# Layer 0's experts: the first product with stationary weights, its output features along the partitions

## The chip, the cores and the metric

The kernel runs on one core of one Trainium2 chip. The metric is the device time of one execution in microseconds (us). The times of the kernel before are those of ten executions: median 4035.64 us, lowest 4032.58, highest 4039.06. The engines are named as in the profile: PE is TensorE's matmul pipe, PEld its weight loads, DVE VectorE, ACT ScalarE, POOL GpSimd, SP SyncE. ACTq and SPq are the queues of ACT and SP where they issue transfers.

## The reference

A graph network with 6250 nodes of 256 features is computed in four parts, each added to the running `x`: a weighted graph convolution with a small dense head, a mixture of eight experts, a relational graph layer, and a second mixture of six experts. The change lies in the second part alone:

```python
def _moe(tokens, router_w, w1, b1, w2, b2):     # tokens: layernorm of x, 6250 x 256
    logits = tokens @ router_w.T
    probs = softmax(logits); rw, re = top_k(probs, 2); rw = rw / rw.sum(-1)
    out = tokens
    for e in range(8):
        h = gelu(tokens @ w1[e] + b1[e], approximate=False)
        y = h @ w2[e] + b2[e]
        out = out + combine[:, e:e + 1] * y
    return out
```

All numbers are float32, and both weight arrays are 8 x 256 x 256.

## The kernel before

The work runs in stages, one after another: lists of edges; messages of the first graph layer; their sums, with the dense head, the router and the sending of tokens woven in; the experts of layer 0; the table of the second graph layer; its sums with the experts of layer 1 woven in; and a last stretch with the remaining experts of layer 1.

**How tokens reach the experts.** The router picks two experts for each token, and each token's row is written by an indirect DMA to two places of an array `xs` in HBM, grouped by expert. Experts' regions are cut into tiles of 128 rows, of which there are at most TE = 105 in all, so every tile belongs to one expert. Which expert it is and where the tile begins in `xs` is known only when the program runs: the numbers are read into registers, eight tiles at a time (`blocks_of`, L1394 and L1395), on SP for the place and on PE and DVE for the expert.

**The stage of the experts (L1384 to L1451).** `in_stages` runs five functions as a software pipeline over the 105 tiles. In round i it calls them from the last to the first, each on an older tile:

- `finish(i-4)`: the second product. The transposed hidden rows are the stationary operand, and the expert's `fw2` (256 columns, at an address from a register) moves. DVE adds the bias `fb2` (L1448), and ACT's queue issues the 128 KB transfer to `ys` (L1449).
- `across(i-3)`: two PE transposes of the hidden rows (L234) and an ACT copy out of PSUM to `fhT` (L236).
- `hidden(i-2)`: the first product. The transposed tokens `fxT` are stationary, `fw1` moves (L1428). DVE adds `fb1` along the free axis (L1432), and ACT applies Gelu to the 128 x 256 result (L1433).
- `into(i-1)`: two PE transposes of the tokens (L234) and an ACT copy to `fxT` (L236).
- `fetch(i)`: SP loads 128 rows of `xs` (L1400).

I write F, A, H and T for the PE work of `finish`, `across`, `hidden` and `into`. A float32 matmul shows in the profile as two MATMUL rows, here called halves: F and H have four halves of 256 columns each. A float32 transpose shows as one row, so A and T have two rows of 128 columns each.

**Buffers.** The pool `experts` has three buffers for each of `fx`, `fxT`, `fh`, `fhT` and two for `fy`. PSUM tiles of F and H come from a pool of four banks, those of A and T from a pool of two.

**What sets the order.** The framework puts each engine's instructions into one list when the program is compiled. It starts from the order in which the program writes them, may put a later instruction ahead of an earlier one that its plan sees waiting, and adds the waits. On the chip each engine goes through its list in order. In the steady part of this stage PE's list is F, A, H, T, as written.

**Around the stage.** Before it, `rows_of("L0_ffn_b1")` and `rows_of("L0_ffn_b2")` (L1305, L1306; DMA issued at L1110) spread the two bias arrays over all partitions. `cols`, a 128 x 48 array that is made at the start of the program, holds other biases and `L0_ffn_b1` as columns, 128 features along the partitions. After the stage, `combine` (L1469, L1475) gathers rows of `ys` with indirect DMAs, adds them to `X`, and the table of the second graph layer (L1509) begins.

Other lines that the prediction uses: L239 (two ACT activations of 128 x 128, one for each half of a PSUM tile that two transposes filled, in the dense head of layer 0), and L246 with L253 and L1091 (the experts of layer 1, whose first two products have the weights stationary and whose last group is a single tile of 128 rows).

Of the kernel before, what the change touches and what calls it, by code (L numbers as in the profile page):

```python
# [8 lines left out]
F32 = mybir.dt.float32  # L9
# [5 lines left out]
AF = mybir.ActivationFunctionType  # L15
# [5 lines left out]
D = 256  # L21
# [19 lines left out]
TE = (2 * N + 8 * 127) // 128  # L41
# [16 lines left out]
def gnn_ffn_kernel(ctx: ExitStack, tc: tile.TileContext, a, out):  # L58
    nc = tc.nc
# [7 lines left out]
    def psum_mm(name):  # L67
        return p_mm.tile([128, 512], F32, tag="mm", name=name)
# [81 lines left out]
    col0, n = {}, 0  # L150
    for name in (
# [8 lines left out]
        k = math.prod(ap.shape) // 128  # L160
# [4 lines left out]
    cols = const.tile([128, 48], F32, name="cols")  # L165
# [5 lines left out]
    def load_w(pool, name, tag=None):  # L171
        w = pool.tile([128, 2, a[name].shape[1]], F32, name=f"w_{name}", tag=tag or f"w_{name}")
        nc.sync.dma_start(w, a[name].rearrange("(k p) f -> p k f", p=128))
        return w

    def blocks_of(blk, t0, engines, top):
        _, v = nc.values_load_multi_w_load_instructions(
            blk[0:1, t0 : t0 + 8],
            engines=engines,
            min_val=0,  # L180
            max_val=top,
            skip_runtime_bounds_check_because="it is counted or bounded",
        )
        return v
# [45 lines left out]
    def transpose_to(name, dest, x, bias=None):  # L230

        pt = p_tr.tile([128, 2, 128], F32, tag="tr", name=f"pt_{name}")
        for k in range(2):
            nc.tensor.transpose(pt[:, k, :], x[:, k * 128 : (k + 1) * 128], ident)  # L234
        if bias is None:
            nc.scalar.copy(dest, pt)  # L236
        else:
            for k in range(2):
                nc.scalar.activation(dest[:, k, :], pt[:, k, :], AF.Relu, bias=bias[k])  # L239
# [23 lines left out]
    w = load_w(xp0, "L0_gnn_W", "x_out")  # L263
# [97 lines left out]
    with tc.If(unsorted > 0):  # L361
        with tc.tile_pool(name="reorder", bufs=1) as rp:
# [3 lines left out]
            for i, (name, dt) in enumerate((("src", I32), ("edge_weight", F32), ("edge_type_8", I32))):  # L366
                e = rp.tile([EP, EC], dt, name=f"e_{name}", tag="e")
# [153 lines left out]
    for b in range(NT):  # L521
        for h in range(2):
# [4 lines left out]
                start=(b == 0),  # L527
                stop=(b == NT - 1),
# [124 lines left out]
    for c0 in range(0, TN, DCH):  # L653
# [21 lines left out]
        for c in range(DCH):  # L675
# [4 lines left out]
                start=(c0 + c == 0),  # L680
                stop=(c0 + c == TN - 1),
# [414 lines left out]
    def load_experts(pool, name):  # L1096
        n_e = a[name].shape[0]
        w = pool.tile([128, n_e, 2, D], F32, name=f"w_{name}")
        for e in range(n_e):
            nc.sync.dma_start(w[:, e], a[name][e].rearrange("(k p) f -> p k f", p=128))  # L1100
        return w


    def rows_of(name, pool):

        v = a[name]
        k = math.prod(v.shape)
        r = pool.tile([128, k], F32, name=f"rows_{name}")
        flat = v.rearrange("(o n) -> o n", o=1) if len(v.shape) == 1 else v.rearrange("e (o n) -> o (e n)", o=1)
        nc.sync.dma_start(r, flat.to_broadcast([128, k]))  # L1110
        return r
# [5 lines left out]
    fw1 = fp.tile([128, 8, 2, D], F32, name="fw1")  # L1117
# [184 lines left out]
        sum_and_send("e", True)  # L1302
    fp2 = ffn0.enter_context(tc.tile_pool(name="ffn0b", bufs=1, side="right"))
    fw2 = load_experts(fp2, "L0_ffn_w2").rearrange("p e k f -> p (e k f)")
    fb1 = rows_of("L0_ffn_b1", fp2)  # L1305
    fb2 = rows_of("L0_ffn_b2", fp2)  # L1306
    fw1 = fw1.rearrange("p e k f -> p (e k f)")

    def in_stages(stages, items):

        held = [None] * len(stages)
        for i in range(len(items) + len(stages) - 1):
            for k in reversed(range(len(stages))):
                if 0 <= i - k < len(items):
                    held[k] = stages[k](*(held[k - 1] if k else items[i]))
# [75 lines left out]
    with tc.tile_pool(name="experts", bufs=3) as xp:  # L1391
        state = {}

        def fetch(i):  # L1394
            if i % 8 == 0:  # L1395
                state["place"] = blocks_of(places, i, [ENG.SP], 8 * CAP)
                state["expert"] = blocks_of(experts, i, [ENG.PE, ENG.DVE], 7)
            e, at = state["expert"][i % 8], state["place"][i % 8]
            x = xp.tile([128, D], F32, name=f"fx{i}", tag="fx")
            nc.sync.dma_start(x, xs[bass.ds(at, 128), :])  # L1400
            if i in (30, 40):
                k = (i - 30) // 10
                nc.scalar.dma_start(
                    wr[:, k], a["L1_gnn_weight"][:, k * 128 : (k + 1) * 128, :].rearrange("r p o -> p r o")
                )
            if i == 50:
                nc.scalar.dma_start(wl, a["L1_gnn_loop_weight"].rearrange("(k p) f -> p k f", p=128))
            if i % 2 == 0 and i // 2 < NT:
                t = i // 2
                nc.gpsimd.tensor_scalar(  # L1410
                    X[:, t, :],
                    X[:, t, :],
                    stretch[:, t : t + 1],
                    offset[:, t : t + 1],
                    op0=OP.mult,
                    op1=OP.add,
                )
            return i, e, x

        def into(i, e, x):  # L1420
            xT = xp.tile([128, 2, 128], F32, name=f"fxT{i}", tag="fxT")
            transpose_to(f"fx{i}", xT, x)
            return i, e, xT

        def hidden(i, e, xT):
            ps = psum_mm(f"pf1_{i}")
            for k in range(2):
                nc.tensor.matmul(  # L1428
                    ps[:, :D], xT[:, k, :], fw1[:, bass.ds(e * 2 * D + k * D, D)], start=(k == 0), stop=(k == 1)
                )  # L1430
            h = xp.tile([128, D], F32, name=f"fh{i}", tag="fh")
            nc.vector.tensor_add(h, ps[:, :D], fb1[:, bass.ds(e * D, D)])  # L1432
            nc.scalar.activation(h, h, AF.Gelu)  # L1433
            return i, e, h

        def across(i, e, h):
            hT = xp.tile([128, 2, 128], F32, name=f"fhT{i}", tag="fhT")
            transpose_to(f"fh{i}", hT, h)
            return i, e, hT

        def finish(i, e, hT):
            ps = psum_mm(f"pf2_{i}")
            for k in range(2):
                nc.tensor.matmul(  # L1444
                    ps[:, :D], hT[:, k, :], fw2[:, bass.ds(e * 2 * D + k * D, D)], start=(k == 0), stop=(k == 1)
                )
            y = xp.tile([128, D], F32, name=f"fy{i}", tag="fy", bufs=2)
            nc.vector.tensor_add(y, ps[:, :D], fb2[:, bass.ds(e * D, D)])  # L1448
            nc.scalar.dma_start(ys[i * 128 : (i + 1) * 128, :], y)  # L1449

        in_stages([fetch, into, hidden, across, finish], [(i,) for i in range(TE)])  # L1451
    ffn0.close()


# [38 lines left out]
    for gi, t, i in tiles:  # L1493
        if i == 0 and gi + 1 < len(TABLE_GROUPS):
            stats[gi + 1] = combine(*TABLE_GROUPS[gi + 1])
        xT = ready.pop(t)
        h = hp.tile([128, NR, 3, D], BF16, name=f"hx{t}", tag="hx")
# [8 lines left out]
        for r in range(0, NR, 2):  # L1506
            ps = psum_mm(f"phx{t}_{r}")
            for k in range(2):
# [4 lines left out]
                    start=(k == 0),  # L1513
                    stop=(k == 1),
# [11 lines left out]
        ps = psum_mm(f"plo{t}")  # L1526
# [219 lines left out]
```

## Time and profile before

| what | value |
|---|---|
| median of ten executions | 4035.64 us |
| the profiled execution | 4036.39 us |
| its span in the profile | 4034.6 us |
| PE busy | 3438.2 us, 85% of the span |
| stage of the experts, first `fx` issue to last `ys` issue | 2020.6 to 2290.2 us, 269.6 us |
| PE busy between 2100 and 2150 us | 48.92 of 50 us |
| DVE, ACT, POOL busy there | 17.42, 21.56, 0 us |
| TensorE clock granted there | 1.00 |
| one tile, steady | 2.36 us |

Times in the profile are microseconds from the start of the span. A row of a timeline gives the start, the time taken, the engine, the line, the operation, the output and the inputs with their shapes, a count, and in brackets how long the engine was idle before and what ended that. A busy share of PE near 100% doesn't say that PE is at its best, since the end of a matmul is modelled and includes the way through the array.

### The profile page before, as it was taken

The numbers are of one execution on the slowest core, as the hardware profiler recorded it, in microseconds if no ns is written. First come the engines' busy times: TensorE is split into PE (matmuls) and PEld (weight loads), VectorE is DVE, ScalarE is ACT, GpSimd is POOL, SyncE is SP. The second block draws the span as 40 slices with busy tenths as digits, with TensorE's granted clock in tenths as the row PEclk, the third lists the DMA queues.
The fourth block names the chain that finished last, engine by engine and source line by source line (L and its number), as shares of the span: only waits on it lengthen the run. The fifth ranks groups of instructions, "written<-read, shape, count | busy, mean of one in ns | idle before, by whom it ended". The sixth has DMA issues, their size and how long they took to land.

```text
span 4034.6 us, 53283 instructions
## 1 busy us (share of the span) xinstructions
PE 3438.2 (85%) x14649; PEld 2300.1 (57%) x14649; DVE 2036.6 (50%) x5609; ACT 1320.0 (33%) x3006; POOL 2252.2 (56%) x2450
## 2 busy tenths in 40 slices
PE   7968877777777688888789779996789999999999
PEld 5756666656666355555467534442456666666556
DVE  6872111111111577777723387664556666666552
ACT  3714333333333233333234335662112222221213
POOL 1007777777777455555420285335777777777740
PEclk9989998998999889999899889997899999999999
DMA  4435333333333555555433354446555555555530
GB/s 122 167 109 169 126 128 126 128 128 129 130 127 124 215 180 191 191 191 191 162 127 109 98 189 196 193 198 219 150 144 151 154 152 153 150 150 150 146 106 9
DMA packets 227434, 602.88 MB, mean 149 GB/s; under 512 B 40620, under 2 KB 121689, under 8 KB 207276
## 3 DMA queue, kind: packets, MB, share of 16 engines
q0 software_dynamic: 100736, 295.11, 23.2%
q1 hardware_dynamic: 108242, 287.41, 20.5%
q10 hardware_dynamic: 18138, 16.68, 1.2%
q8 instruction: 132, 2.16, 0.2%
q14 instruction: 186, 1.52, 0.1%
HBM read 362.97 MB, written 236.11 MB: 148 GB/s over the span
## 4 chain that ended last, share of the span: by engine, by line
PE 46%; DVE 14%; DMA 8%; issue 6%; POOL 3%; ACT 2%; DVEq 1%; POOLq 0%; ACTq 0%; SPq 0%
PE ph_e1a L246 6%; DMA msgs<-msgn,at 6%; PE pa1a L1012 6%; PE py1a L1091 6%; PE ph_e2a L246 5%; PE pxn L908 4%; DVE acc L985 4%; PE pa0e L983 4%; PE phx L1509 4%; PE pf L1428 2%; PE pf L1444 2%; DVE rest L1519 2%; POOL msgs L926 1%; DVE acc L1016 1%; PE pt_fh L234 1%
## 5 line engine op out<-in xcount | busy, mean ns | idle before, releaser
L1004 POOL DMA_INDIRECT g1a<-hx,idxT x830 | 826.2, 995 | 322.6 <-PE pa1a L1012 146.5
L908 PE MATMUL pxn<-acc,sTn 128*128 x3128 | 795.2, 415 | 238.9 <-DVE sTn L891 230.7
L926 POOL DMA_INDIRECT msgs<-msgn,at x782 | 783.0, 1001 | 270.6 <-DMA msgs<-msgn,at 138.1
L908 PEld LDWEIGHTS pxn<-acc,sTn 128*128 128x128 f32 x3128 | 618.2, 207 | 415.0 <-DVE sTn L891 264.6
L983 PE MATMUL pa0e<-g0e,m0e 128*128 128x256 f32 x1660 | 482.3, 425 | 132.5 <-POOL m0e L970 64.6
L923 ACT ACTIVATE msgn<-pxn,ewT 128x256 f32<-128x256 f32 x782 | 370.1, 473 | 645.9 <-PE pxn L908 487.3
L1016 DVE TENSOR_TENSOR acc<-acc,pa1a 128x256 f32 x830 | 347.3, 418 | 343.4 <-PE pa1a L1012 312.0
L983 PEld LDWEIGHTS pa0e<-g0e,m0e 128*128 128x128 f32 x1660 | 284.4, 201 | 295.8 <-issue 117.0
L899 DVE COPY msgn<-srcT 128x32 f32<-128x32 f32 x98 | 18.1, 188 | 825.6 <-DMA msgs<-msgn,at 709.2
L1012 PE MATMUL pa1a<-g1a,m1a 128*128 128x256 bf16 x2490 | 375.4, 283 | 54.1 <-DMA g1a<-hx,idxT 38.5
L985 DVE TENSOR_TENSOR acc<-acc,pa0e 128x256 f32 x830 | 347.6, 419 | 142.3 <-PE pa0e L983 100.9
L970 POOL TENSOR_SCALAR m0e<-minus,keye 128x128 f32<-128x128 f32 x414 | 250.7, 621 | 280.8 <-PE pa0e L983 127.8
L1012 PEld LDWEIGHTS <-m1a 128*128 128x128 bf16 x2490 | 243.5, 100 | 277.2 <-issue 191.1
L1509 PE MATMUL phx<-wr,xT 128*128 128x512 f32 x784 | 369.2, 615 | 28.7 <-DVE rest L1519 20.8
L1091 PE MATMUL py1a<-w_L_ffn_expert_w,v2a 128*128 128x256 f32 x1176 | 285.5, 383 | 6.0 <-DVE acc L1016 3.0
L246 PE MATMUL ph_e1a<-xT3a,w_L_ffn_expert_w 128*128 128x512 f32 (+2 forms) x672 | 289.1, 557 | 0.0
L253 ACT ACTIVATE v1a<-ph_e1a,cols 128x512 f32<-128x512 f32 (+2 forms) x168 | 106.5, 634 | 539.3 <-PE ph_e1a L246 539.1
L246 PE MATMUL ph_e2a<-v1a,w_L_ffn_expert_w 128*128 128x512 f32 (+2 forms) x672 | 280.0, 542 | 2.1 <-DVE acc L1016 1.3
L1509 PEld LDWEIGHTS phx<-wr,xT 128*128 128x128 f32 x784 | 148.2, 197 | 189.1 <-issue 162.7
L1469 POOL DMA_INDIRECT y<-ys,ats x98 | 96.6, 986 | 277.9 <-issue 263.4
L1091 PEld LDWEIGHTS py1a<-w_L_ffn_expert_w,v2a 128*128 128x128 f32 x1176 | 208.4, 190 | 43.8 <-ACT v2a L253 10.1
L1092 DVE SCALAR_TENSOR_TENSOR X<-py1a,C1a,X 128x256 f32<-128x256 f32 x294 | 139.1, 482 | 111.4 <-PE py1a L1091 110.4
(649 smaller groups left out, 4325.9 us busy)
## 6 DMA issues: line engine op xcount, KB each, us to landing
g0e<-msgs SPq DMA_DIRECT2D x104, 1040.0 KB
hx<-hx SPq DMA_DIRECT2D x49, 1536.0 KB
rowsn<-lane_rows SPq DMA_DIRECT2D x98, 256.0 KB
fx<-xs SPq DMA_DIRECT2D x105, 128.0 KB
ys<-fy ACTq DMA_DIRECT2D x105, 128.0 KB
g1a<-hx,idxT POOLq DMA_INDIRECT x830, 3.1
msgs<-msgn,at POOLq DMA_INDIRECT x782, 2.4
msgs<-none SPq DMA_DIRECT2D x10, 650.0 KB
```

The source lines that it names most:

```text
L246: nc.tensor.matmul(ps[:, :ncols], w[:, k, f * 128 : (f + 1) * 128], xT[:, k, :ncols], start=(k == 0), stop=(k == 1),)
L908: nc.tensor.matmul(come, sT[:, k, j, :], acc[:, bass.ds(blocks[j] * D + k * D, D)], start=(k == 0), stop=(k == 1),)
L923: nc.scalar.activation(msg[:, j, :D], come, AF.Copy, scale=ewT[:, t0 + j : t0 + j + 1])
L926: ins = nc.gpsimd.indirect_dma_start(out=msgs, out_offset=bass.IndirectOffsetOnAxis(ap=at[:, t0 + j : t0 + j + 1], axis=0), in_=msg[:, j, ...
L970: nc.gpsimd.tensor_scalar(m[:, j], minus, key[:, j : j + 1], None, op0=OP.is_equal)
L983: nc.tensor.matmul(ps[:, :D], m[:, j, :], g[:, j, :D], start=True, stop=True)
L985: nc.vector.tensor_add(here, here, ps[:, :D])
L1004: nc.gpsimd.indirect_dma_start(out=g, out_offset=None, in_=table, in_offset=bass.IndirectOffsetOnAxis(ap=idxT[:, t0 + j : t0 + j + 1], axi ...
L1012: nc.tensor.matmul(ps[:, :D], m[:, j, :], g[:, k * D : (k + 1) * D], start=(k == 0), stop=(k == 2))
L1016: nc.vector.tensor_add(here, here, ps[:, :D])
L1091: nc.tensor.matmul(ps[:, :D], hT[:, k, j : j + 128], w[:, k, :], start=(k == 0), stop=(k == 1))
L1509: nc.tensor.matmul(ps, xT[:, k, :], wr[:, k, r : r + 2, :].rearrange("p r o -> p (r o)"), start=(k == 0), stop=(k == 1),)
```

## The change

`hidden` takes the weights as the stationary operand and the transposed tokens as the moving one, so that its result has features along the partitions, in two blocks of 128 features by 128 tokens in one PSUM tile. That is the form in which `finish` needs it: `across` is gone, with its two transposes and its copy. The bias now stands along the partitions, so ACT's Gelu takes it as its bias operand, reads PSUM itself and writes `fhT`, in two instructions, one for each block; the DVE add and the array `fb1` are gone. The stationary operand is no longer read at an address from a register: `into` copies the expert's weights (128 x 512) and its two bias columns (128 x 2) with DVE into tiles of their own, `fw` and `fb`, three buffers each.

```diff
@@ -1302,7 +1302,6 @@
     fw2 = load_experts(fp2, "L0_ffn_w2").rearrange("p e k f -> p (e k f)")
-    fb1 = rows_of("L0_ffn_b1", fp2)
     fb2 = rows_of("L0_ffn_b2", fp2)
@@ -1420,22 +1419,28 @@
         def into(i, e, x):
             xT = xp.tile([128, 2, 128], F32, name=f"fxT{i}", tag="fxT")
             transpose_to(f"fx{i}", xT, x)
-            return i, e, xT
-
-        def hidden(i, e, xT):
+            b1 = xp.tile([128, 2], F32, name=f"fb{i}", tag="fb")
+            nc.vector.tensor_copy(b1, cols[:, bass.ds(e * 2 + col0["L0_ffn_b1"], 2)])
+            w = xp.tile([128, 2 * D], F32, name=f"fw{i}", tag="fw")
+            nc.vector.tensor_copy(w, fw1[:, bass.ds(e * 2 * D, 2 * D)])
+            return i, e, xT, w, b1
+
+        def hidden(i, e, xT, w, b1):
             ps = psum_mm(f"pf1_{i}")
-            for k in range(2):
-                nc.tensor.matmul(
-                    ps[:, :D], xT[:, k, :], fw1[:, bass.ds(e * 2 * D + k * D, D)], start=(k == 0), stop=(k == 1)
-                )
-            h = xp.tile([128, D], F32, name=f"fh{i}", tag="fh")
-            nc.vector.tensor_add(h, ps[:, :D], fb1[:, bass.ds(e * D, D)])
-            nc.scalar.activation(h, h, AF.Gelu)
-            return i, e, h
-
-        def across(i, e, h):
+            for f in range(2):
+                for k in range(2):
+                    nc.tensor.matmul(
+                        ps[:, f * 128 : (f + 1) * 128],
+                        w[:, k * D + f * 128 : k * D + (f + 1) * 128],
+                        xT[:, k, :],
+                        start=(k == 0),
+                        stop=(k == 1),
+                    )
             hT = xp.tile([128, 2, 128], F32, name=f"fhT{i}", tag="fhT")
-            transpose_to(f"fh{i}", hT, h)
+            for f in range(2):
+                nc.scalar.activation(
+                    hT[:, f, :], ps[:, f * 128 : (f + 1) * 128], AF.Gelu, bias=b1[:, f : f + 1]
+                )
             return i, e, hT
@@ -1448,7 +1453,7 @@
-        in_stages([fetch, into, hidden, across, finish], [(i,) for i in range(TE)])
+        in_stages([fetch, into, hidden, finish], [(i,) for i in range(TE)])
```

More of the change, by code (lines that the diff above doesn't have):

```diff
@@ L1422, in into @@
             transpose_to(f"fx{i}", xT, x)
-            return i, e, xT
-        def hidden(i, e, xT):
-            ps = psum_mm(f"pf1_{i}")
-            for k in range(2):
-                nc.tensor.matmul(
-                    ps[:, :D], xT[:, k, :], fw1[:, bass.ds(e * 2 * D + k * D, D)], start=(k == 0), stop=(k == 1)
-                )
-            h = xp.tile([128, D], F32, name=f"fh{i}", tag="fh")
-            nc.vector.tensor_add(h, ps[:, :D], fb1[:, bass.ds(e * D, D)])
-            nc.scalar.activation(h, h, AF.Gelu)
-            return i, e, h
-        def across(i, e, h):
-            hT = xp.tile([128, 2, 128], F32, name=f"fhT{i}", tag="fhT")
-            transpose_to(f"fh{i}", hT, h)
+            b1 = xp.tile([128, 2], F32, name=f"fb{i}", tag="fb")
[4 more added lines that the diff above has]
+        def hidden(i, e, xT, w, b1):
+            ps = psum_mm(f"pf1_{i}")
+            for f in range(2):
[7 more added lines that the diff above has]
+                    )
+            hT = xp.tile([128, 2, 128], F32, name=f"fhT{i}", tag="fhT")
+            for f in range(2):
+                nc.scalar.activation(
+                    hT[:, f, :], ps[:, f * 128 : (f + 1) * 128], AF.Gelu, bias=b1[:, f : f + 1]
+                )
             return i, e, hT
```

## The prediction

> **What bounds the kernel now.** The page comes first. PE is the busiest engine, and in the chain that ended last the two products of the experts (L1428, L1444) have 4% of the span and the transposes of `fh` (L234) 1% more.
>
> ```profile
> PE 3438.2 (85%) x14649; PEld 2300.1 (57%) x14649; DVE 2036.6 (50%) x5609; ACT 1320.0 (33%) x3006; POOL 2252.2 (56%) x2450
> ```
>
> Then the stage's own windows (length, busy time of PE, PEld, DVE, ACT, POOL, granted clock, DMA share, GB/s):
>
> ```profile
> 2100.00:2150.00 50.00, 48.92 (x246) 36.67 (x247) 17.42 (x41) 21.56 (x61) 0.00 (x0) 1.00 0.35 111
> ```
>
> PE is full, at full clock; DVE and ACT are idle for over half, POOL wholly. The next stage gathers from `ys` and begins after the last `ys` transfer, so what the stage gains or loses passes on whole. The timeline of one steady tile shows how:
>
> ```profile
> 2274.05 0.38 PE L234 MATMUL pt_fx<-ident,fx 128*128 128x128 f32 x2
> 2274.27 1.03 PE L1444 MATMUL pf<-w_L_ffn_w,fhT 128*128 x4
> 2274.32 0.42 DVE L1432 TENSOR_TENSOR fh<-pf,rows_L_ffn_b 128x256 f32<-128x256 f32 x1 [0.91 <-PE pf L1428]
> 2274.79 0.42 ACT L1433 ACTIVATE fh<-fh 128x256 f32<-128x256 f32 x1
> 2275.26 0.20 PEld L234 LDWEIGHTS pt_fh<-ident,fh 128*128 128x128 f32 x2 [0.37 <-ACT fh L1433]
> 2275.27 0.44 PE L234 MATMUL pt_fh<-ident,fh 128*128 128x128 f32 x2
> 2275.54 1.03 PE L1428 MATMUL pf<-fw,fxT 128*128 x4
> 2276.41 0.38 PE L234 MATMUL pt_fx<-ident,fx 128*128 128x128 f32 x2
> ```
>
> Take differences of PE's starts: T 0.22, F 0.86, a hole of 0.14, A 0.27, H 0.87: 2.36 us. The hole is A waiting for Gelu (2274.79 + 0.42 = 2275.21): add and Gelu stand one after the other between H and A. A takes 0.27 where T takes 0.22, since PE refills after a wait: 0.05.
>
> One other wait is regular, once in eight tiles (waits in 2045 to 2290: total us, times, longest):
>
> ```profile
> PEld pf L1428 <- DVE fy L1448: 7.7, 13, 0.6
> ```
>
> These are the tiles where new registers are read.
>
> **The change part by part.**
>
> *A goes*: 0.27 + 0.14 = 0.41 per tile on PE, all on the path. Its ACT copy goes too, on an engine that waits anyway.
>
> *H turns*: eight halves of 128 columns instead of four of 256. The last group of layer 1 has this form:
>
> ```profile
> 4007.60 1.05 PE L246 MATMUL ph_e1a<-xT3a,w_L_ffn_expert_w 128*128 128x128 f32 x8
> 4008.31 0.75 ACT L253 ACTIVATE v1a<-ph_e1a,cols 128x128 f32<-128x128 f32 x2 [2.16 <-PE ph_e1a L246]
> 4009.70 0.62 ACT L253 ACTIVATE v2a<-ph_e2a,cols 128x128 f32<-128x128 f32 x2 [0.64 <-PE ph_e2a L246]
> 4010.12 1.13 PE L1091 MATMUL py1a<-w_L_ffn_expert_w,v2a 128*128 128x256 f32 x4 [0.23 <-ACT v2a L253]
> ```
>
> Eight halves end after 1.05; one takes 0.27, so the pitch is (1.05 - 0.27) / 7 = 0.111 and H takes 0.89, 0.02 more than now. PE's work per tile becomes 0.22 + 0.86 + 0.89 = 1.97.
>
> The rows above show eight weight loads hidden behind eight halves. The Trainium skill ("TensorE: Matmul & The Clock Gate", sections "Back-to-back issue gap" and "LDWEIGHTS") speaks against the change: the spacing of load and matmul is set by both, short moving operands pay more per column, and loading 128 columns costs about 128/1.2 = 107 ns. If each load stood in line with its half, an estimate from that page is 0.85 more per tile and about 86 us for the stage.
>
> *Gelu reads PSUM, twice.* An activation of 128x128 from PSUM with a bias column takes 0.36 (L239 361 ns, L253 363 to 367), the second following 0.26 after the first (0.62 for two). Gelu in this form is not in the trace: its cost lies between 0.36 and the 0.42 of today's 128x256 Gelu; I take 0.36, the same shape, source and bias. Both wait for the whole of H, by this pair from the dense head, where two transposes fill the halves of one PSUM tile and one activation reads each:
>
> ```profile
> 1607.98 0.63 PE L234 MATMUL pt_h7e<-ident,h7e 128*128 128x128 f32 x2
> 1608.65 1.72 ACT L239 ACTIVATE uTe<-pt_h7e,b_mlp 128x128 f32<-128x128 f32 x5 [8.58 <-PE pt_h7e L234]
> ```
>
> ACT, idle for 8.58, starts 0.04 after the second transpose ends (1608.61), not after the first (1608.40). So with H starting at 0: H ends 1.05, first Gelu 1.09 to 1.45, F 0.06 later (v2a to py1a: 4009.70 + 0.36 to 4010.12) at 1.51. F begins with its first half, for which one Gelu is enough: py1a started at 4010.12, before the second v2a ended (4009.70 + 0.62 = 4010.32). The second Gelu ends at 1.71, before F's second pair (1.94). After H, PE has only T, until 1.11. **The new wait is 0.40 before F, with 0.05 of refill.**
>
> *Queued behind it.* On PE, behind F, the next H. On ACT, behind Gelu, the copy to `fxT` for which the next H waits: it would start at about 1.61 and end by 2.0, in time for an H at 2.4. ACT's list also holds the `ys` issue, which waits for DVE's add: F ends its issue as H starts, its data come 0.16 later, the add takes 0.43, the issue follows 0.12 later and takes 0.33: 1.04, just before Gelu at 1.09. ACT's sum is 0.27 + 0.52 + 0.33 = 1.12 per tile.
>
> *DVE's copies.* 128x512 lies between two rows: 188 ns for 128x32 (L899) and this one; by a straight line 0.42.
>
> ```profile
> L568 DVE COPY pos<-nowhere 128x784 f32<-128x784 f32 x1 | 0.6, 553 | 0.0
> ```
>
> The bias copy is like `share` (L1218), 0.17. With the add of `fy` 0.43, DVE has 1.02 per tile, hidden by PE's 1.97; H waits for the copy, which is written one round ahead. If the copy came late, 0.42 per tile would be open. POOL has no work there after 2041.
>
> *Nothing*: `fb1`'s load (two SP issues, 0.99 together, for both biases, at 1994.57; SP's next issue is at 2015.96) and the transfers (256 KB per tile, 109 GB/s now, 125 then; a `ys` transfer lands 1.70 after its issue, two buffers).
>
> *Reading registers* costs 13 x 0.6 = 8 now. PE keeps them for F alone, DVE gets more. I leave it at 8, with 0 and 16 as ends.
>
> *Where the hole goes.* In PE's written order F, H, T a tile takes 1.97 + 0.40 + 0.05 = 2.42, more than now. But the lists are planned ahead and the plan fills holes it sees. At the start of this stage it did:
>
> ```profile
> 2035.14 1.03 PE L1444 MATMUL pf<-w_L_ffn_w,fhT 128*128 x4
> 2036.00 1.03 PE L1428 MATMUL pf<-fw,fxT 128*128 x4
> 2036.87 0.38 PE L234 MATMUL pt_fh<-ident,fh 128*128 128x128 f32 x2
> ```
>
> An H stands ahead of an A, written before it. Today's steady hole (0.14) was left; 0.40 is three times that. Once one T is taken early, the next H is ready when its predecessor ends, and the list becomes H1 H2 F1 T F2 H3 T T F3: only before F3 is there a hole, 1.51 - 0.89 - 0.44 = 0.18, with refill 0.23 in three tiles: (3 x 1.97 + 0.23) / 3 = 2.05. Today's 0.14 shows that plan and chip differ by about 0.1; once in three tiles that is 0.03. **I take 2.08.**
>
> The first tiles stay as they are: until 2039.84 DVE's add of `fy` waits for a `ys` transfer of 7.33 that lies beside the loads of `wr`. Some 101 tiles remain: (2.36 - 2.08) x 101 = 28, and the pipeline is one step shorter at the end (today 4.3 from the last H to its add), 1. The sum is -29 from the profiled execution's 4036.4, thus 4007.4; the median of the runs lies 0.75 below that execution, so **4007**.
>
> **The rivals.**
> - *All holes filled*: 1.97 to 2.00, -37 to -41: 3996. For it: four PSUM banks and three buffers. Against: today's 0.14 stays open.
> - *Half the gain*: only T is brought forward and 0.18 + 0.05 stays in each tile: 2.20, -17: 4019.
> - *The order stays*: 2.42, (+0.06 x 101) - 1 = +5: 4041. With Gelu at 0.42, 2.48 and +11: 4047. For it: one order for 100 tiles today. The change then does what it says on PE and gives it back as a wait.
> - *Slower*: the order stays and F waits for both Gelus at its first matmul: at 1.77, hole 0.66, tile 2.68, +0.32 x 101 - 1 = +31: 4067. It decides once hole and refill exceed the 0.41 - 0.02 that PE saves. Against: the py1a row.
> - *Weight loads not hidden*: 0.19 each (PEld rows of L246), H 1.52, tile 2.60, +24: 4060. Against: the ph_e1a row.
>
> **How the numbers follow.** Forecast (-15 to -36) 0.45; all filled 0.12; half 0.17; order stays 0.16 (of which 0.04 above +8); slower 0.07; loads 0.03. About 0.2% (8 us) is what a measurement of this kernel can tell from none. Faster 0.74, within 0.12, slower 0.14. The range goes from 3994 (PE's bare work, -41) to 4044 (order kept), and leaves out 0.14 above and 0.03 below.
>
> **What would show it.** Rows of `fh` transposes gone; H as x8 with about 0.89 to what follows; two Gelus starting 0.04 to 0.1 after H's end; F's wait on ACT in a third of the tiles only; two H one after the other in PE's list; tiles 2.05 to 2.1 apart. Wrong if F waits about 0.4 in every tile, if H waits for DVE's copies, or if H's pitch is near 0.19.

## The result, and the profile after

The changed kernel takes 4058.54 us (median of 8 executions, 4056.80 to 4060.06) beside 4035.36 of the kernel before (28 executions): a ratio of 1.0059, 95% interval 1.005 to 1.0067. It is slower by 23 us, where 28 less were forecast; the time lies above the range (3994 to 4044). Its profiled execution took 4057.59 with a span of 4055.8, 21.2 more than the span before.

The steady window of the stage, in the columns shown for before:

```profile
2100.00:2150.00 50.00, 43.99 (x278) 37.29 (x277) 20.26 (x59) 17.55 (x60) 0.00 (x0) 1.00 0.34 105
```

PE was full there; now it is idle for 6 of 50 us, at the same full clock. The timeline of one tile shows where:

```profile
2152.37 1.13 PE L1449 MATMUL pf<-w_L_ffn_w,fhT 128*128 x4 [0.30 <-ACT fhT L1441]
2152.46 0.37 ACT L236 COPY fxT<-pt_fx 128x256 f32<-128x256 f32 x1
...
2153.33 1.05 PE L1432 MATMUL pf<-fxT,fw 128*128 128x128 f32 x8
...
2154.22 0.38 PE L234 MATMUL pt_fx<-ident,fx 128*128 128x128 f32 x2
2154.43 0.43 DVE L1425 COPY fw<-fw 128x512 f32 x1 [0.47 <-PE pf L1432]
2154.49 0.63 ACT L1441 ACTIVATE fhT<-pf,fb 128x128 f32<-128x128 f32 x2 [1.65 <-PE pf L1432]
2154.91 0.73 PEld L1449 LDWEIGHTS pf<-w_L_ffn_w,fhT 128*128 128x128 f32 x4 [0.54 <-ACT fhT L1441]
2154.91 1.13 PE L1449 MATMUL pf<-w_L_ffn_w,fhT 128*128 x4 [0.30 <-ACT fhT L1441]
```

Differences of PE's starts again: F 0.96, H 0.89, T 0.22 and a hole of 0.47 behind T: 2.54. The order is F, H, T as written. H ends its halves at 2153.33 + 1.05 = 2154.38, the first Gelu starts 0.11 later (0.10 in the median of all tiles), and F 0.42 after that. ACT had been idle for 1.65 before the Gelu, so ACT is not what is late: the hole is the latency of H's end, one Gelu, and the way to F, with only T to cover it. The waits between 2045 and 2300 us say the same for nearly all tiles (us in total, times, longest):

```profile
PEld pf L1449 <- ACT fhT L1441: 53.8, 99, 1.2
...
PE pf L1449 <- ACT fhT L1441: 30.4, 97, 1.0
```

The second place is the start of the stage: DVE and POOL in 2014 to 2041.5, then PE.

```profile
2015.97 24.35 DVE L1423 COPY fb<-cols 128x2 f32 x1 [3.70 <-DMA xs<-toke,ats]
2040.23 0.41 DVE L1425 COPY fw<-fw 128x512 f32 x1
```

```profile
2014.59 26.72 POOL L1409 TENSOR_SCALAR X<-X,stretch,offset 128x256 f32<-128x256 f32 x49
```

```profile
2022.71 1.24 PE L234 MATMUL pt_fx<-ident,fx 128*128 128x128 f32 x4 [9.04 <-DMA fx<-xs]
2040.79 2.05 PE L1432 MATMUL pf<-fxT,fw 128*128 128x128 f32 x8 [16.84 <-DVE fw L1425]
```

The first copy of two bias columns, 0.17 in the median of all tiles, took 24.35 while POOL ran the 49 scalings of `X` (0.55 each) that `fetch` contains and that the plan puts in one row. PE had the first transposed rows at 2024 and stood 16.84 for the copy of the weights queued behind it.

The account, by the two profiles: the first add of `fy` starts at 2045.44 instead of 2031.47 (+14.0), the last `ys` store at 2311.7 instead of 2290.2 (+21.5), and the span grew by 21.2. So 14.0 comes at the start and 7.5 between the first add and the end. In the steady part the adds are 2.545 apart on average (94 of them, 2061.9 to 2298.5), before 2.437 (98, 2048.3 to 2284.8; the 2.36 of a plain tile and the register readings): +0.108 x 93 = +10.0. The remaining -2.5 lies in the first tiles: from the first add to the seventh it is 16.4 now and was 19.2 before. What makes that difference was not traced.

### The profile page after: what moved, and what is told of

Its sections match the earlier page's. It is cut to its first block, busy times and chain, and to the rows that moved or that the text cites. A ratio compares the mean times of both kernels' runs of the same rounds, so it can differ in the third digit from the quotient of the medians.

```text
span 4055.8 us, 53391 instructions
## 1 busy us (share of the span) xinstructions
PE 3415.2 (84%) x14859; PEld 2304.7 (57%) x14859; DVE 2077.7 (51%) x5714; ACT 1304.0 (32%) x3006; POOL 2257.1 (56%) x2450
## 3 DMA queue, kind: packets, MB, share of 16 engines
q0 software_dynamic: 100736, 295.11, 23.1%
## 4 chain that ended last, share of the span: by engine, by line
PE 46%; DVE 14%; DMA 11%; issue 7%; POOL 3%; ACT 3%; DVEq 1%; POOLq 0%; ACTq 0%; SPq 0%
DMA msgs<-msgn,at 9%; PE ph_e1a L246 6%; PE pa1a L1012 6%; PE py1a L1091 6%; PE ph_e2a L246 5%; PE pxn L908 5%; PE phx L1514 4%; DVE acc L985 4%; PE pa0e L983 4%; PE pf L1449 3%; PE pf L1432 2%; POOL msgs L926 1%; DVE rest L1524 1%; DVE acc L1016 1%; ACT fhT L1441 1%
## 5 line engine op out<-in xcount | busy, mean ns | idle before, releaser
L899 DVE COPY msgn<-srcT 128x32 f32<-128x32 f32 x98 | 17.9, 186 | 827.5 <-DMA msgs<-msgn,at 737.6
L253 ACT ACTIVATE v1a<-ph_e1a,cols 128x512 f32<-128x512 f32 (+2 forms) x168 | 106.4, 634 | 537.9 <-PE ph_e1a L246 537.8
```

## The experiments

Two theories were set up. **Start:** SBUF work of DVE that comes up while POOL's series runs is held up by that series. **Steady:** the plan keeps F, H, T, so F waits in every tile for a Gelu that starts only when the whole of H is done. The rival to the second was that the added DVE copies cost the time in the steady part too.

The runs were made on several chips. On two of them the kernel before takes 4340 (e1 to e4) and 4331 us (c1, e5 to e7), with executions up to 1% apart and a mean granted clock of about 0.91; on the chips of c2, e8, e9 and e10 it takes 4033 to 4035, at 0.93. In the windows of the steady part that were read, the granted clock is 1.00 on both kinds. So each ratio is to the kernel before on the same chip, and theories are judged by stage times in each run's profile: us after the start of the last scattering DMA of the tokens (`xs`, L1259), and the mean distance of the `fy` adds in the steady part.

| kernel | median us | ratio, 95% interval | first H | first fy | last ys | tile |
|---|---|---|---|---|---|---|
| before | 4035.36 | 1 | 11.1 | 17.9 | 276.6 | 2.44 |
| after | 4058.54 | 1.0059, 1.005 to 1.0067 | 27.2 | 31.9 | 298.1 | 2.54 |
| c1_after_again | 4342.83 | 1.0021, 1.0007 to 1.0035 | 10.4 | 15.1 | 281.4 | 2.54 |
| c2_before_look | 4034.24 | one execution | 11.1 | 17.8 | 276.4 | 2.44 |
| e1_scale_on_dve | 4346.64 | 1.0015, 0.9995 to 1.0034 | 23.1 | 26.8 | 293.2 | 2.54 |
| e2_no_copies | 4350.37 | 1.0030, 1.001 to 1.0049 | 10.5 | 22.9 | 290.6 | 2.54 |
| e3_copies_only | 4335.60 | 0.9992, 0.9973 to 1.001 | 27.2 | 33.9 | 284.5 | 2.36 |
| e4_h_first | 4323.06 | 0.9965, 0.9945 to 0.9985 | 27.4 | 33.0 | 269.2 | 2.23 |
| e5_two_banks | 4301.07 | 0.9934, 0.9915 to 0.9954 | 14.9 | 21.7 | 251.3 | 2.19 |
| e6_first_on_act | 4344.17 | 1.0023, 1.001 to 1.0037 | 10.7 | 30.0 | 297.1 | 2.54 |
| e7_order_and_act | 4303.90 | 0.9922, 0.99 to 0.9945 | 10.7 | 19.1 | 248.5 | 2.20 |
| e8_scale_on_act | 4047.78 | 1.0035, 1.0021 to 1.0049 | 17.0 | 21.7 | 288.6 | 2.55 |
| e9_five_stages | 3992.38 | 0.9896, 0.9881 to 0.9911 | 17.1 | 22.8 | 230.1 | 1.98 |
| e10_order_alone | 3987.10 | 0.9883, 0.9867 to 0.99 | 14.9 | 22.0 | 228.6 | 1.98 |

Against the kernel before, the totals of e1 to e4 are 4 to 12 us lower than their last `ys` stores say. The stage times are those of one execution each, and the kernel before has no profile from that chip, so why is not settled.

### POOL's series given to DVE (e1)

```diff
-                nc.gpsimd.tensor_scalar(
+                nc.vector.tensor_scalar(
                     X[:, t, :], ...
```

> The changed kernel with one edit: the 49 scalings of X at the start of the experts' stage run on DVE instead of POOL. Theory P (a DVE copy from SBUF to SBUF can't run while POOL works, so the first H waits for the end of POOL's 26.7 us): the first H comes back to about 2025 us, and the total falls by 13 to 16, to about 4044 (ratio to before 1.002). Rival Q (the first copies wait for something else, such as the first reading of registers): the first H stays near 2041 and the total near 4058. Both expect 2.54 us per steady tile.

The copies ran at their own times (the first `fb` 0.17, `fw` 0.43) and the first H followed the first T by 1.3 us. But the plan put the scalings on DVE ahead of the tables of places and experts, so the first row of tokens was loaded 12.6 us later (19.5 instead of 6.9), which neither theory had foreseen. The tile stayed at 2.54. For the start the run shows that the copies are short once POOL is quiet, not what that would save.

### No copies (e2)

```diff
-            nc.vector.tensor_copy(b1, cols[:, bass.ds(e * 2 + col0["L0_ffn_b1"], 2)])
...
-            nc.vector.tensor_copy(w, fw1[:, bass.ds(e * 2 * D, 2 * D)])
+            s = i * 8 // TE
+            b1 = cols[:, s * 2 + col0["L0_ffn_b1"] : s * 2 + col0["L0_ffn_b1"] + 2]
+            w = fw1[:, s * 2 * D : (s + 1) * 2 * D]
```

> The changed kernel without DVE's copies: the weights and the bias column are read in place at fixed addresses, expert i*8//105 for tile i, so the choice of the expert in the first product is left out. Theory P: first H near 2025, and the tile stays at 2.54, so about 4044. Rival R (the copies also cost time in each steady tile): the tile falls to 2.36 to 2.42 and the total to about 4028 to 4034. Rival Q would leave the first H late only if what delays it isn't the copies: about 4058.

This kernel leaves out the choice of the expert in the first product. The tile stayed at 2.54: **the copies are not what costs in the steady part**, and that rival falls. The first H came at 10.5, near the 11.1 of the kernel before. The first add came late all the same, and DVE's timeline shows why:

```profile
2147.71 16.09 DVE L1376 TENSOR_SCALAR by<-ats,moves 128x98 f32<-128x98 int32 x2 [1.16 <-DVE moves L1371]
```

This is a step of the shift of the places (`by` and `to`); two such rows in one took 0.45 to 0.59 before the change. With no copies it was the next DVE work on SBUF to meet POOL's series, and it was held up in their stead.

### The copies alone, on the kernel before (e3)

The five stages and the first product of the kernel before are kept; only its weights are copied by DVE to a tile of their own first.

```diff
-                    ps[:, :D], xT[:, k, :], fw1[:, bass.ds(e * 2 * D + k * D, D)], start=(k == 0), stop=(k == 1)
+                    ps[:, :D], xT[:, k, :], w[:, k * D : (k + 1) * D], start=(k == 0), stop=(k == 1)
```

> The kernel before with one part of the change alone: DVE copies the expert's 128x512 weights into a tile (two buffers), and the first product, tokens still stationary, reads that tile. Theory P: the first H comes 14 to 16 later than before, the steady tile keeps its 2.36 to 2.44, total about 4047 to 4051. Rival Q: within 3 us of before, 4033 to 4039.

The first copy of the weights took 24.61, and the first H came at 27.2: the loss at the start belongs to the copies and POOL's series, whatever form H has. The tile fell to 2.36, that of a plain tile before, and the stall of H at register readings, up to 0.6 once in eight tiles, no longer stands among its waits: the first product is not read at an address from a register any more. The gain of 0.08 per tile (8 us in all) and the late start (16) leave 7.9 at the last store; the total shows no difference from the kernel before, where 11 to 15 us more were expected.

### H ahead of F (e4)

```diff
-            for k in reversed(range(len(stages))):
+            later = held[2]
+            for k in (2, 3, 1, 0):
                 if 0 <= i - k < len(items):
-                    held[k] = stages[k](*(held[k - 1] if k else items[i]))
+                    got = later if k == 3 else held[k - 1] if k else items[i]
+                    held[k] = stages[k](*got)
```

> The changed kernel with one edit: in each round the program writes H of tile i-2 before F of tile i-3, so that PE has F and T between an H and the F that needs its Gelu. Theory S (the steady loss is the wait of F for Gelu, 0.47 and a refill of 0.1 in each tile): the tile falls from 2.54 to about 2.0, the start stays late, total about 4058 - 0.5 x 100 = 4005 to 4010. Rival (the loss lies in H's own pitch, in the copies or in transfers): the tile stays above 2.4, total above 4040.

```profile
2260.79 1.03 PE L1451 MATMUL pf<-w_L_ffn_w,fhT 128*128 x4
2261.66 1.05 PE L1434 MATMUL pf<-fxT,fw 128*128 128x128 f32 x8
2262.55 1.03 PE L1451 MATMUL pf<-w_L_ffn_w,fhT 128*128 x4
2263.41 0.60 PE L234 MATMUL pt_fx<-ident,fx 128*128 128x128 f32 x4
2264.26 1.16 PE L1434 MATMUL pf<-fxT,fw 128*128 128x128 f32 x8 [0.24 <-ACT fxT L236]
```

In PE's rows F follows H after 0.89, as fast as H's halves are issued: **the wait for Gelu is gone, and only the order was edited.** The plan then set T in pairs, and every second H waited for ACT's copy of the second T (45 times in 200 us), so the tile stopped at 2.23, where about 2.0 was expected, and the total at 0.35% below the kernel before instead of 0.7%.

### The changed kernel once more (c1)

> The changed kernel itself, beside the others on one chip. If the change costs the same everywhere, the ratio to the kernel before is again near 1.006 (first measurement 1.0059), the first product H of the first expert tile starts some 27 us after the issue of the last scattering DMA of the tokens (before: 11), and an expert tile takes 2.55 us (before: 2.45). If the ratio is far from 1.006 on another chip while these stage times are the same, totals of different chips cannot be set against each other and only the stage times can.

Tile 2.54 again, but the ratio is 1.0021 where 1.006 was expected, and the start was not late:

```profile
2152.91 0.26 DVE L1423 COPY fb<-cols 128x2 f32 x1 [2.42 <-issue]
2153.07 0.89 DVE L1425 COPY fw<-fw 128x512 f32 x1
```

The copy came 1.39 us after POOL's series began (2151.52), in the first profile 1.38 after, and got through at once. So the start's loss is not fixed: two profiles of one program differ by 16.8 us in their first H, and theory P of e1, that a copy can't run while POOL works, is too strong. The chip alone does not decide it either: e5, e6 and e7 ran on the chip of c1 and had long DVE rows (11.61, 25.06 and 13.37). POOL pays when DVE gets in: its 49 scalings took 28.39 here and 26.72 there.

### A PSUM tile for each half of H (e5)

```diff
-            ps = psum_mm(f"pf1_{i}")
+            ps = [psum_mm(f"pf1_{i}"), psum_sm(f"pf1b_{i}")]
```

> Each half of the first product gets a PSUM tile of its own, so the first Gelu waits for two matmuls and not for all four. Theory (the hole of 0.47 ahead of F is the Gelu chain: .11 + .36 to the first F weights, begun only when the whole of H is done, with only T of .22 beside it): the first Gelu starts .22 sooner, so the hole ahead of F falls by up to .22 with the same order of F, H and T, and the tile falls from 2.55 to about 2.3; the listing order may also shift, since half tiles are smaller pieces. The start stays late (first H about 27 us after the last scattering DMA). Total about 25 us less than the changed kernel, ratio to the kernel before about 1.000. Rival (F waits for the second Gelu, or the hole comes from something other than the joint wait): the tile stays at 2.5 and the ratio at 1.006.

The tile fell further than expected (2.19 instead of 2.3), but the run does not measure the joint wait by itself: the plan now also took halves of the next H ahead of F, so order and wait changed together. These rows show the part of the joint wait (`pf` is the tile of the first half, `pf1b` that of the second):

```profile
2301.74 0.61 PE L1432 MATMUL pf<-fxT,fw 128*128 128x128 f32 x4
...
2302.18 0.83 PE L1432 MATMUL pf1b<-fxT,fw 128*128 128x128 f32 x6
2302.38 0.37 ACT L1441 ACTIVATE fhT<-pf,fb 128x128 f32<-128x128 f32 x1 [0.96 <-PE pf L1432]
```

The Gelu on the first tile starts at 2302.38, after its own four halves end (2302.35) and while those of the second tile are still running. The ratio is 0.9934 where 1.000 was expected; part of that is the start, since the first copy was held up for only 11.61 us in this run and the first H came at 14.9 and not at 27.

### The first copies on ScalarE (e6)

```diff
-            nc.vector.tensor_copy(b1, ...)
+            copy = nc.scalar.copy if i < 10 else nc.vector.tensor_copy
+            copy(b1, ...)
...
```

The copy of the weights is changed in the same way.

> ScalarE makes the copies of the bias columns and of the weights for the first 10 expert tiles, while POOL scales X; from the tenth tile on VectorE makes them as in the changed kernel. Theory (the late start is VectorE's SBUF copies standing behind POOL's scalings): first H 11 to 13 us after the last scattering DMA instead of 27, with the expert tile at 2.55 as before; the first fy addition at 18 to 23 us instead of 32, because the kernel without the copies showed VectorE's shift of the places itself held up by POOL until +17; total 9 to 14 us less than the changed kernel, ratio to the kernel before about 1.003. Rival (the late start is where the planner puts H or POOL's own work that holds up the loads): first H stays at 27 and the total at that of the changed kernel.

The first H came at 10.7 as expected, but the first add at 30.0, not 18 to 23, and the total is that of the changed kernel on the same chip (1.0023 and 1.0021):

```profile
2143.88 25.06 DVE L1376 TENSOR_SCALAR by<-ats,moves 128x98 f32<-128x98 int32 x2 [0.56 <-DVE moves L1371]
```

The shift of the places was now held up until 0.4 us before the end of POOL's series, with the add of `fy` behind it on DVE. Moving the copies alone only moves the victim.

### The order H, T, F (e7)

```diff
+            for k in (2, 1, 3, 0):
...
-            xT = xp.tile([128, 2, 128], F32, name=f"fxT{i}", tag="fxT")
+            xT = xp.tile([128, 2, 128], F32, name=f"fxT{i}", tag="fxT", bufs=4)
```

with the first copies on ScalarE as in e6.

> The stages are listed in the order H, T, F in each round instead of F, H, T, so that a whole tile of TensorE's work stands between a tile's H and its F; the transposed rows have four buffers instead of three, since H, T, F needs one more in flight; and the first copies are on ScalarE as in the run beside this one. Theory: no wait for a Gelu is left, the tile is TensorE's work alone, F .86 + H .89 + T .22 = 1.97 to 2.05, the first H comes at 11 to 13 us, and the last ys store at about 18 + 100 x 2.03 + 12 = 233 to 245 us after the last scattering DMA (changed kernel 298, before 277): 32 to 44 us less than before, ratio about .990 to .993. Rival (another engine or the loads of fx bound the tile): the tile stops at 2.25, as in the kernel with H ahead of F, and the ratio is about .996.

No wait for a Gelu was left, and the total is lower by 0.78%, inside the theory's range of ratios, but the last store came at 248.5, not 233 to 245, and the tile took 2.20, not 1.97 to 2.05:

```profile
2301.12 0.63 ACT L1444 ACTIVATE fhT<-pf,fb 128x128 f32<-128x128 f32 x2 [1.31 <-PE pf L1435]
...
2301.64 0.37 ACT L236 COPY fxT<-pt_fx 128x256 f32<-128x256 f32 x1
...
2302.06 0.97 PEld L1435 LDWEIGHTS pf<-fxT,fw 128*128 128x128 f32 x8 [0.36 <-ACT fxT L236]
```

A T written one round ahead of its H is evacuated behind the two Gelus of the tile before, and H waits for that copy. This is the rival's answer, another engine that bounds the tile, at nearly its size (2.25). The start helped the total: the shift was held up for 13.37 us here, against 25.06 in e6, and the first add came at 19.1 instead of 30.0.

### The kernel before, once more (c2)

> The kernel before, for its stage times beside the runs of this chip. If the total alone depends on the chip, its stages are those of the first profile: first fy addition 18 us after the issue of the last scattering DMA, last ys store at 277 us, 2.45 us for an expert tile, VectorE's shift of the places done within 4 us because it had begun before POOL's series of scalings. If it is VectorE's luck against POOL's series that differs from run to run, this kernel is hardly touched by it: only the last pair of the shift could be held up, and nothing waits for VectorE until the first product.

Stage times within 0.4 us of the first profile's. The shift ran from 2013.99 to 2018.2 although POOL's series began at 2015.7: its steps were under way before the series, and took 0.59 and 0.78 beside it instead of 0.45 and 0.56. What held DVE's copies up for 24 us only slowed these.

### POOL's series given to ScalarE (e8)

```diff
-                nc.gpsimd.tensor_scalar(
+                nc.scalar.activation(
+                    X[:, t, :], X[:, t, :], AF.Identity, bias=offset[:, t : t + 1], scale=stretch[:, t : t + 1]
```

> The 49 scalings of X are ScalarE's instead of POOL's, so POOL has no compute beside the expert tiles at all; the copies stay on VectorE. Theory (VectorE's SBUF operations that come up while POOL's series runs may be held up to its end, in some executions and not in others): with the series gone no copy of the bias or the weights and no step of the shift takes over 1 us, in this run or in any. The price is 49 x about .4 = 20 us of ScalarE, which stands ahead of its first copy of the transposed rows, so first H comes at 10 to 16 us after the last scattering DMA and the first fy at 15 to 20; the tile stays at 2.54, last ys store at 282 to 287 us (kernel before 277): ratio to the kernel before 1.001 to 1.003. Rival (the wait has nothing to do with POOL's scalings): a copy of the bias or a step of the shift of over 10 us is there again.

The first copies ran at their own times:

```profile
2017.89 0.17 DVE L1418 COPY fb<-cols 128x2 f32 x1 [3.70 <-DMA xs<-toke,ats]
2018.04 0.43 DVE L1420 COPY fw<-fw 128x512 f32 x1
```

No DVE copy took over 0.43 us and no pair of shift steps over 0.55. The three profiles without POOL's series (e1, e8, e9) have no long row; of the nine in which the copies or the shift first came up during it (after, c1, e2 to e7, e10), c1 alone has none. So the series is the cause of the long rows. ACT's own row of scalings (40 of them in 19.75) held up the loads instead, by 6.6 us: ACT issues half of the stores of zeros to `xs` (L1362), the last of which came 11.7 us after the last scattering DMA instead of 4.1, and the loads came behind them. That is more than expected (first H at 17.0 instead of 10 to 16, last store 288.6 instead of 282 to 287), and the tile is as slow as ever.

### Five stages, T two rounds ahead (e9, e10)

```diff
+            was = list(held)
+            for k in (3, 4, 1, 2, 0):
                 if 0 <= i - k < len(items):
-                    held[k] = stages[k](*(held[k - 1] if k else items[i]))
+                    held[k] = stages[k](*(was[k - 1] if k else items[i]))
...
-            xT = xp.tile([128, 2, 128], F32, name=f"fxT{i}", tag="fxT")
+            xT = xp.tile([128, 2, 128], F32, name=f"fxT{i}", tag="fxT", bufs=4)
             transpose_to(f"fx{i}", xT, x)
+            return i, e, xT
+
+        def weights(i, e, xT):
             b1 = xp.tile([128, 2], F32, name=f"fb{i}", tag="fb")
...
-        in_stages([fetch, into, hidden, finish], [(i,) for i in range(TE)])
+        in_stages([fetch, into, weights, hidden, finish], [(i,) for i in range(TE)])
```

e9 has it on top of e8, e10 on the changed kernel as it is.

> As the run before, with the order of the stages mended: five stages in place of four, listed in each round as H, F, T, copies, fetch, so that the transposition of a tile's rows is two rounds ahead of its H, with four buffers for them, and F of the tile before and T stand between H and its F. In the kernel with the order H, T, F a tile took 2.19 with no wait for a Gelu left, but H waited .36 for ScalarE's copy of the transposed rows behind the two Gelus. Theory: that wait goes too, and the tile is TensorE's work alone, F .86 + H .89 + T .22 = 1.97; first fy at 15 to 20 us after the last scattering DMA, last ys store at 18 + 105 x 1.97 + 5 = 225 to 235 us (kernel before 277), total 42 to 50 us less than before, ratio .989 to .991. Rival (H waits for something else in its turn, or the loads or stores of the rows are what bounds it): the tile stays at 2.15 to 2.2 and the ratio at .992 to .994.

> The five stages in the order H, F, T, copies, fetch alone: POOL scales X as in the changed kernel, and VectorE makes all copies. Theory (the two losses are separate and add up): the tile is 1.97 as in the run with the scalings on ScalarE, and the start is the changed kernel's, with VectorE's first copy held up by anything from 0 to 25 us behind POOL's series; first fy 15 to 33 us after the last scattering DMA, last ys store at 105 x 1.97 + 3 = 210 us after it, so at 225 to 243 us (kernel before 276, changed kernel 298 where the copy was held up for 24): 33 to 51 us less than before, ratio .987 to .992, and the lower end only where the copy is not held up. Rival (the late copies also upset the order, so that the two losses do not add up): the tile is above 2.1 or the last store later than 250 us.

The steady window and PE's rows of e10:

```profile
2100.00:2150.00 50.00, 50.00 (x354) 46.14 (x353) 25.93 (x76) 25.51 (x77) 0.00 (x0) 1.00 0.43 135
```

```profile
2100.85 1.06 PE L1436 MATMUL pf<-fxT,fw 128*128 128x128 f32 x8
2101.74 1.03 PE L1453 MATMUL pf<-w_L_ffn_w,fhT 128*128 x4
2102.61 0.38 PE L234 MATMUL pt_fx<-ident,fx 128*128 128x128 f32 x2
2102.82 1.06 PE L1436 MATMUL pf<-fxT,fw 128*128 128x128 f32 x8
```

H 0.89, F 0.87, T 0.21: 1.97, PE without a gap, and no wait of PE in the list of waits. The totals of e9 and e10 are 3992.4 and 3987.1, ratios 0.9896 and 0.9883, thus 40.9 and 48.2 us less than the kernel before on the same chips; by the last `ys` store it is 46.5 and 48.0 (276.6 less 230.1 and 228.6). Tile and ratio lie in the ranges expected of both; e9's first add (22.8) came later than expected and its gain falls 1 us short. **These beat both kernels, e10 with nothing moved off POOL.** In e10's profile the first copy was held up for 11.59 us; the intervals of e9 and e10 overlap, so which start is better is not shown. Nor was the old form of the first product run in a better order: its own PE work, from the rows before, is T 0.22, F 0.86, A 0.22 to 0.27 and H 0.87, together 2.17 to 2.22. By this estimate the turned product is worth 0.20 to 0.25 of the 0.46 per tile between 2.44 and 1.98, and the rest is the waits that went with the order and the register readings.

## Why the prediction was wrong, step by step

**PE's bare work, right.** A gone, H 0.89 with a pitch of 0.111 and weight loads hidden, T 0.22, F 0.86: 1.97, and e9 and e10 run at 1.98. The estimate from the Trainium skill of loads in line with their halves (0.85 more per tile) is not borne out. The rival of the weight loads falls.

**Gelu, right in size.** Two in 0.63, and F's first half waits for the first alone, so the rival "F waits for both" falls too. The start after H's end was mis-sized: 0.11, where 0.04 was read off a transpose. The first four tiles have the 0.04, the steady ones 0.10; what adds the 0.06 is not shown. A nearer row had it: the first four halves of `ph_e1a`, whose PSUM tile the first L253 activation reads, end at 4008.21, and it starts at 4008.31.

**"Where the hole goes", the first step that failed.** The forecast rested on the plan bringing the next H ahead of F: 2.08 per tile. It brought T three rounds ahead of its written place in PE's list, and H never. The evidence was one H ahead of an A at the start of the stage, where DVE's add of `fy` waited for a late `ys` transfer; the steady order of 100 tiles, with a hole of 0.14 left open, was the better witness and had been put down as a rival at 16%. With that rival's own sum, 2.42, the tile is 2.54: 0.07 more from Gelu's start, and 0.05 more from PE's refill, since F after the wait takes 0.96 and not 0.91. So a wait of F in every tile, which the forecast had in one tile of three, stood in the place of the gain: 0.18 lost per plain tile, where 0.28 was to be won. The order is shown as the cause by e4, e9 and e10. What the plan's estimate of the hole was, and so why it left H, stays open.

**"DVE's copies ... hidden", the second.** The sum of DVE's work is right (0.43 + 0.17 + 0.43 per tile) and hidden in the steady part (e2). But the sentence "POOL has no work there after 2041" was taken as an all-clear, though it says that POOL has work until 2041, and the first copies fall due at 2016. The first of them took 24.35 where 0.17 was put down. "The first tiles stay as they are" failed with it: +14 in the profiled execution. The question was not whether DVE has the time but what else is on SBUF when it first runs.

**"Reading registers", mis-sized.** It was left at 8 us; e3 shows that the copies take it away, 0.08 per tile, nearly all of the 8. In the changed kernel this gain is part of the average of 2.545.

**The sum.** Forecast -28 and -1; it came to +10.0 in the steady part (with the register readings' gain in it), +14.0 at the start, -2.5 not traced: 21.5. The range's upper end was "the order stays" without a late start. In c1, with a quiet start, the last `ys` store came 4.8 later than before (281.4 less 276.6) and the ratio was 1.0021, 8.5 us on 4035: by either, an estimate of 4040 to 4044, near the rival's 4041. So how far the time lay above the range was a matter of the start, which is not the same in every profile, but the sign was not: neither measurement of the changed kernel is faster than the kernel before, and that is the order's doing.

## What to carry to other kernels

A step that shortens an engine's work can show nothing, or a loss as here, until the order of that engine's list covers the new latency: write the order so that one whole tile of other work stands between producer and consumer, and don't count on a planner to find it. Here that was worth 60 us between the first add and the last store (266.3 in the changed kernel, 206.6 in e10). When work is moved to DVE, look up in the profile what POOL does at the moment of its first instruction, not only in the steady part. A fix that takes one victim out of the way of a series can hand the wait to the next, as in e2 and e6. Moving the series itself took the long rows away (e8), at a price elsewhere.

## What was not expected of the hardware

DVE's SBUF instructions were held up by POOL's series of 49 SBUF scalings in very different measure: a copy of 128x2 for 24.35 (after), 24.53 (e4), 11.59 (e10) and not at all (c1, 0.26); the shift step for 25.06 (e6), 16.09 (e2) and 13.37 us (e7). They end 0.4 to 1.0 us before the series does (after, e3, e4, e6) or at some point inside it, after which both engines go on, with some of POOL's scalings slower (e10: 0.78 instead of 0.55). In c1, e10 and the first profile the copy came up at the same point of the series (1.39, 1.38 and 1.38 us after its start), in e4 and e5 too (1.37 and 1.38), so what decides it is not seen; it stays open. DVE's additions of `fh` and `fy`, which read PSUM, took 0.43 and 0.42 beside the same series in the kernel before (2026.80 and 2031.47), and so did a conversion from SBUF to SBUF, `ats` from `to` (L1381), in 0.30 at 2027.14: not every SBUF instruction of DVE is held up.

The Trainium skill ("SBUF — State Buffer", section "Who interferes with whom") says that a DVE instruction in a two-port mode and a GpSimd instruction exclude each other, and that the one that issues first has the shared ports for that whole instruction. The long rows look like such blocking: a copy of 0.17 took 24.35. Whether these DVE instructions ran in such a mode, no trace here shows. The wait is also longer than one instruction: a scaling takes 0.55, and here a copy stood through up to 45 of them. Of such a series that section says nothing.
